# A product moved from VectorE to GpSimd, and the last values of a layer in one go, in a four-layer sparse graph network

## The chip, the cores and the metric

The kernel runs on one core of a Trainium2 chip. The metric is the device time of the whole program in microseconds, the median over several executions. One further execution was recorded by the hardware profiler; durations of single instructions come from it.

## The reference

The input is a matrix of 3327 nodes by 256 features and an adjacency matrix of 3327 x 3327 integers, of which about one in 208 is 1. Four layers follow each other, all with the same adjacency. Layer 0:

```
h = x @ Wt.T + bt                              # 64 features
s = leaky_relu(h @ Wa.T + ba, 0.2)
w = softmax(where(adj > 0, s, NEG), axis=1)
y = x + (w @ h) @ Wp.T + bp
x = gamma * layernorm(y) + beta
```

Layers 1 to 3, each with its own weights, 8 heads of 32:

```
q, k, v = layernorm(x) @ w_qkv
attn = softmax(where(adj != 0, q @ k.T * SCALE, -inf))
x = x + (attn @ v) @ w_proj + b_proj
x = x + gelu(layernorm(x) @ w1 + b1) @ w2 + b2     # 1024 inner features
```

## The kernel before

The nodes are 26 blocks of 128 rows (the last is short), in groups of four. The work has two phases.

**Layer 0 with the lists (0 to about 500 us).** For every block, SyncE loads 128 rows of the adjacency as integers (`load`), ScalarE turns them into bf16 zeros and ones (`sign`, L714, after a one-column MEMSET of the padding, L711, on VectorE for the first three blocks and on GpSimd from then on), TensorE transposes them and ScalarE copies the transposes (`turn`, L723 and L724), and TensorE multiplies h with them (`sums`). From the same bf16 rows VectorE makes the lists of neighbours: `candidates` multiplies the row by the numbers 1 to 208 within each of 16 segments (L731, the product `v` of 128 x 3328, two buffers), takes the eight largest of each segment (L735, 16 MAX8), and `list` adds the segment's offset to those that are above zero (L741, L742) and draws the 40 largest by five MAX8 and four MATCH_REPLACE8 (L746, L748). The groups' own steps (`copy`, `back`, `soft`, `mix`, `project`, `add`, `norm`, `norm1`, `turn1`, `qkv`, `store`) are laid out by hand in a table `plan` of two places for each block; the loop issues, for block i, the load and sign of block i+2, the even place of the plan, `candidates(i)`, the turn of block i+2, the odd place, and `list(i)`. `soft` begins with a count and a comparison that writes `OH` (L892). Each engine runs its instructions in the order in which the code issues them.

**Layers 1 to 3.** The nodes are sorted by degree, so block 0 has lists of 40 and the others of 24 down to 10 (`CAPS`). `ORDER` takes them alternately from both ends, and block 0 last. `CHUNK` joins them in chunks of 3, then fours, then 2 and at last block 0 alone. Each block is cut in groups of four list places. GpSimd issues one indirect DMA for each place (L1303), which fetches 128 rows of keys and values of 2 KB; ten groups are in flight (`NBUF`). On VectorE a group's `scores` are a product and a reduction (L1325, L1326); after the last group of a block `softmax` takes the maximum and ScalarE the exponent (L1340), and the next block's q is copied by ScalarE (L1311). A group's `values` are a product on VectorE (L1366, three buffers `vw`) that TensorE adds up by transposing matmuls (L1372). Values run a set number of groups behind their block's last scores:

```
for _ in range(2 if len(todo) > NBUF // 2 or b == 0 else 1):
    if todo and wait[todo[0][0]] > 1:
        value()
self.some()
```

`some` issues steps of the rest: `short` are those of one block (copy of the transposes L1390, projection L1396, `add` L1400), `long` those of a chunk, in the order in which chunks become due (normalisation, `up` L1439, `gelu` L1445, `down` L1462, `shift`, `back`, `add` L1480, and, if there is a next layer, its normalisation, q, k and v L1492, and `keep` L1498 to L1500, which copies k and v, scales q, and stores k and v). A rate sets how many `long` steps one call issues. After the scores of the last block the remaining values are drained with a call of `some` after each, then all steps that are left. The next layer's first gather waits until all k and v are stored.

Of the kernel before, what the change touches and what calls it, by code (L numbers as in the profile page):

```python
# [8 lines left out]
FP = mybir.dt.float32  # L9
BF = mybir.dt.bfloat16  # L10
I32 = mybir.dt.int32
AF = mybir.ActivationFunctionType
ALU = mybir.AluOpType
# [4 lines left out]
P = 128  # L18
N = 3327
D = 256  # L20
HEADS = 8
# [11 lines left out]
NB = (N + P - 1) // P  # L33
# [16 lines left out]
NSEG = 16  # L50
SEG = NB * P // NSEG
# [472 lines left out]
def sparse_path(ctx, tc, ins, out, dram, flag):  # L524
    nc = tc.nc
    const = ctx.enter_context(tc.tile_pool(name="s_const", bufs=1))
    small = ctx.enter_context(tc.tile_pool(name="s_small", bufs=4))

    ident = const.tile([P, P], FP, name="s_ident")
# [12 lines left out]
    kv = {1: dram.tile([PADDED + 1, KVW[1]], FP, name="kv1"),  # L542
          2: dram.tile([PADDED, KVW[2]], FP, name="kv2"),
          3: dram.tile([PADDED, KVW[3]], FP, name="kv3")}
# [78 lines left out]
    with tc.tile_pool(name="a", bufs=1) as a, tc.tile_pool(name="aw", bufs=2) as aw, \  # L623
# [10 lines left out]
        seg1 = a.tile([P, SEG], BF, name="seg1")  # L634
# [13 lines left out]
        num = a.tile([P, P], FP, name="num")  # L648
# [3 lines left out]
        part = a.tile([P, 1], FP, name="part")  # L652
# [27 lines left out]
        nd = LMAX + 1  # L680
# [3 lines left out]
        OH = a.tile([P, NB, nd], BF, name="OH")  # L684
# [9 lines left out]
        class Block:  # L694
# [21 lines left out]
            def turn(self, aT):  # L716

                i = self.i
                for k0 in range(0, NB, 7):
# [3 lines left out]
                        nc.tensor.transpose(pt[:, m, :], self.abf[:, k * P:(k + 1) * P], ident_bf)  # L723
                    nc.scalar.copy(aT[:, k0:k0 + len(ks), :], pt[:, :len(ks), :])  # L724

            def candidates(self, part=None):

                i = self.i
                if not part:
                    v = self.v = aw.tile([P, NSEG, SEG], BF, tag="v", name=f"s_v_{i}")  # L730
                    nc.vector.tensor_mul(v, self.abf.rearrange("p (s c) -> p s c", c=SEG),  # L731
                                         seg1[:, None, :].to_broadcast([P, NSEG, SEG]))
                    self.cand = aw.tile([P, NSEG, 8], FP, tag="cand", name=f"cand_{i}")
                for s in range(NSEG) if part is None else range(part * 4, part * 4 + 4):
                    nc.vector.max(out=self.cand[:, s, :], in_=self.v[:, s, :])  # L735

            def list(self):

                i, cand = self.i, self.cand
                tmp = aw.tile([P, NSEG, 8], FP, tag="ctmp", name=f"ctmp_{i}")  # L740
                nc.vector.scalar_tensor_tensor(tmp, cand, 0.0, off, ALU.is_gt, ALU.mult)  # L741
                nc.vector.tensor_add(tmp, cand, tmp)  # L742
                c2 = tmp.rearrange("p a b -> p (a b)")
                for k in range(0, LMAX, 8):
                    top = lists[:, i, k:k + 8]
                    nc.vector.max(out=top, in_=c2)  # L746
                    if k + 8 < LMAX:
                        nc.vector.match_replace(out=c2, in_to_replace=top, in_values=c2,  # L748
                                                imm_value=0.0)
# [91 lines left out]
        class Group:  # L841
# [36 lines left out]
            def soft(self):  # L878


                g, n, b0 = self.g, self.n, self.blocks[0]

                def sv(name):
                    t = aw.tile([P, 4], FP, tag="s_" + name, bufs=1, name=f"s_{name}_{g}")
                    return t[:, :n]

                sg = S.s[:, b0:b0 + n]
                dg = deg[:, b0:b0 + n]
                nc.vector.tensor_copy(dg, self.acc[:, :n, H0])
                top = sv("top")  # L890
                nc.vector.tensor_scalar(top, dg, float(LMAX), None, ALU.min)
                nc.vector.tensor_tensor(OH[:, b0:b0 + n, :],  # L892
                                        num[:, None, :nd].to_broadcast([P, n, nd]),
                                        top[:, :, None].to_broadcast([P, n, nd]), ALU.is_equal)

                at = places[:, :4 * nd].rearrange("p (b k) -> p b k", k=nd)
                for j in range(n):
                    i = b0 + j
                    add = [(tri, i)] + [(ones_bf, k) for k in range(b0, i)]
                    if g:  # L900
                        add += [(rest_tri, i - 4)] + [(ones_bf, k) for k in range(i - 3, b0)]
                    for lhsT, m in add:
                        nc.tensor.matmul(at[:, j, :], lhsT, OH[:, m, :], start=False, stop=True,
                                         skip_group_check=True)
                non, ga, fa, m1, m0, tt, mx = (
                    sv(k) for k in ("non", "ga", "fa", "m1", "m0", "tt", "mx"))
                nc.vector.tensor_scalar(non, dg, -1.0, float(N), ALU.mult, ALU.add)
                nc.vector.tensor_scalar(ga, dg, 0.0, None, ALU.is_gt)
                nc.vector.tensor_scalar(fa, non, 0.0, None, ALU.is_gt)
                nc.vector.tensor_scalar(tt, ga, -NEG0, NEG0, ALU.mult, ALU.add)  # L910
                nc.vector.tensor_mul(m1, sg, ga)
                nc.vector.tensor_add(m1, m1, tt)
                nc.vector.tensor_scalar(tt, fa, -1.0, 1.0, ALU.mult, ALU.add)
                nc.vector.tensor_mul(m0, sg, tt)
                nc.vector.scalar_tensor_tensor(m0, fa, NEG0, m0, ALU.mult, ALU.add)
                nc.vector.tensor_max(mx, m1, m0)
                nc.vector.tensor_sub(m1, m1, mx)
                nc.vector.tensor_sub(m0, m0, mx)
                nc.scalar.activation(m1, m1, AF.Exp)
                nc.scalar.activation(m0, m0, AF.Exp)  # L920
                self.non, self.m1, self.m0, self.tt = non, m1, m0, tt
# [107 lines left out]
        blk = [Block(i) for i in range(NB)]  # L1029
# [28 lines left out]
        for g in range(NG):  # L1058
            x_turn(g)
            if g:  # L1060
                h_of(g - 1)
            if g == 2:
                turn(3)
            if g == 4:
                blk[4].load()
                blk[4].sign()
            for _ in range(2 if g > 3 else 1):
                pieces.pop(0)()
        h_of(NG - 1)
# [34 lines left out]
        def step(g, name):  # L1104
            G = groups[g]
            G.qkv(int(name[3:])) if name[:3] == "qkv" else getattr(G, name)()

        for i in range(4, NB):
            if i + 2 < NB:
                blk[i + 2].load()  # L1110
                blk[i + 2].sign()
            for s in plan[2 * i]:
                step(*s)
            blk[i].candidates()
            if i + 2 < NB:
                turn(i + 2)
                if i % 2 or i + 2 == NB - 1:
                    sums(i + 2)
            for s in plan[2 * i + 1]:
                step(*s)  # L1120
            blk[i].list()
# [77 lines left out]
        top = a.tile([1, nd], FP, name="top")  # L1199
# [77 lines left out]
    class Layer:  # L1277
# [133 lines left out]
        def chunk(self, blocks, n2):  # L1411
            L, w, nxt = self.L, self.w, self.nxt
            n = len(blocks) * P
            b0 = blocks[0]
            x = [t2[:, b, :D] for b in blocks]
            js = range(len(blocks))
            c = {}
# [77 lines left out]
            def keep(j):  # L1495
                b = blocks[j]
                kvr = work.tile([P, 2 * D], FP, tag="kvr", name=f"kvr_{L}_{b}")
                nc.scalar.copy(kvr, c["pk", j])  # L1498
                nc.scalar.mul(t2[:, b, D:2 * D], c["pq", j][:, :D], -HD ** -0.5)
                nc.scalar.dma_start(kv[L + 1][b * P:(b + 1) * P, :], kvr)  # L1500

            def store(j):
                b = blocks[j]
# [50 lines left out]
                self.short.pop(0)()  # L1554

        def run(self):
            for _ in range(NBUF):
                self.issue()
            self.take_q(ORDER[0])

            todo, wait = [], {}

            def value():
                if todo[0][1] == 0:
                    self.weights(todo[0][0])
                self.values(*todo.pop(0))

            for k, b in enumerate(ORDER):
                for g in slots[b]:
                    self.scores(*g)  # L1570
                    if g == slots[b][-1]:
                        self.softmax(b)
                        if k + 1 < NB:
                            self.take_q(ORDER[k + 1])
                    for i in wait:
                        wait[i] += 1
                    for _ in range(2 if len(todo) > NBUF // 2 or b == 0 else 1):
                        if todo and wait[todo[0][0]] > 1:
                            value()
                    self.some()  # L1580
                todo += slots[b]
                wait[b] = 0
            while todo:
                value()
                self.some()
            self.rate = 4.0
            while self.short or self.long:
                self.some()
# [45 lines left out]
```

## Time and profile before

| | us |
|---|---|
| median of 3 runs | 3145.98 (3143.37 to 3151.08) |
| the profiled execution | 3158.07 |
| its span, first to last instruction | 3156.3 |
| VectorE busy | 1935.3 (61%) |
| TensorE busy, mean granted clock | 1794.0 (57%), 0.735 |
| GpSimd busy | 1362.7 (43%) |
| ScalarE busy | 774.6 (25%) |
| gathers of GpSimd (L1303) | 1344 of 947 ns |

Shares are averages over stages with different limits: in the first 500 us GpSimd has next to nothing to do, and in the layers it issues gathers. What a change in one stage is worth is read from that stage alone. A matmul's end is modelled[...].

### The profile page before, as it was taken

The numbers are of one execution on the slowest core, as the hardware profiler recorded it, in microseconds if no ns is written. First come the engines' busy times: TensorE is split into PE (matmuls) and PEld (weight loads), VectorE is DVE, ScalarE is ACT, GpSimd is POOL, SyncE is SP. The second block draws the span as 40 slices with busy tenths as digits, with TensorE's granted clock in tenths as the row PEclk, the third lists the DMA queues.
The fourth block names the chain that finished last, engine by engine and source line by source line (L and its number), as shares of the span: only waits on it lengthen the run. The fifth ranks groups of instructions, "written<-read, shape, count | busy, mean of one in ns | idle before, by whom it ended". The sixth has DMA issues, their size and how long they took to land.

```text
span 3156.3 us, 24036 instructions
## 1 busy us (share of the span) xinstructions
PE 1794.0 (57%) x7561; PEld 1163.5 (37%) x7561; DVE 1935.3 (61%) x3983; ACT 774.6 (25%) x1316; POOL 1362.7 (43%) x1458
## 2 busy tenths in 40 slices
PE   4767752255666666671457667666713435665556
PEld 3645531133333333350334333433512323433334
DVE  6688995457657656533656756755446556656554
ACT  4455621012222222230112212222300111212112
POOL 4000004545555554305555555544054555565550
PEclk9868766577787886785578778878755766776768
DMA  5334306645555565415455555555064554554560
GB/s 207 131 117 148 129 31 204 174 138 169 165 172 162 156 174 152 112 51 177 141 156 156 163 160 150 175 152 140 24 189 125 156 155 135 169 163 147 161 156 13
DMA packets 144486, 453.80 MB, mean 144 GB/s; under 512 B 29521, under 2 KB 40156, under 8 KB 141021
## 3 DMA queue, kind: packets, MB, share of 16 engines
q0 software_dynamic: 113056, 370.26, 40.9%
q1 hardware_dynamic: 9834, 53.90, 4.9%
q10 hardware_dynamic: 21458, 28.02, 2.5%
q8 instruction: 61, 1.00, 0.1%
q14 instruction: 77, 0.63, 0.1%
HBM read 420.64 MB, written 31.42 MB: 143 GB/s over the span
## 4 chain that ended last, share of the span: by engine, by line
DVE 25%; issue 18%; PE 18%; another core or an unknown queue 17%; POOL 11%; ACT 5%; DMA 5%; DVEq 0%; ACTq 0%; POOLq 0%; SPq 0%
POOL kv L1303 11%; DVE kv L1325 5%; DMA kv<-kv,t 4%; DVE sc L1326 3%; DVE vw L1366 3%; PE pu L1439 3%; PE po L1372 3%; PE py L1462 2%; DVE cand L735 2%; PE pk L1492 1%; PE s_pk L1010 1%; ACT s_aT L724 1%; DVE s_v L731 1%; PE pf L591 1%
## 5 line engine op out<-in xcount | busy, mean ns | idle before, releaser
L1303 POOL DMA_INDIRECT kv<-kv,t x1344 | 1273.0, 947 | 1210.3 <-issue 534.2
L1372 PE MATMUL po<-s_ident,vw 128*128 128x128 f32 x2688 | 475.4, 334 | 580.2 <-DVE vw L1366 387.2
L1372 PEld LDWEIGHTS po<-s_ident,vw 128*128 128x128 f32 x2688 | 395.5, 174 | 724.1 <-issue 373.5
L1325 DVE TENSOR_TENSOR kv<-kv,q 128x1024 f32<-128x1024 f32 (+3 forms) x363 | 413.1, 1138 | 397.1 <-ACT q L1311 274.6
L1366 DVE TENSOR_TENSOR vw<-kv,w 128x1024 f32<-128x1024 f32 x333 | 371.4, 1128 | 87.2 <-remote 84.6
L1326 DVE TENSOR_REDUCE sc<-kv 128x32 f32<-128x1024 f32 (+3 forms) x363 | 414.1, 1141 | 12.4
L1439 PE MATMUL pu<-fT,s_w 128*128 128x512 f32 (+3 forms) x768 | 341.2, 579 | 62.3 <-issue 35.8
L1462 PE MATMUL py<-gT,s_w 128*128 128x512 f32 (+2 forms) x672 | 321.8, 597 | 58.1 <-issue 50.2
L1400 DVE TENSOR_TENSOR t<-t,po 128x256 f32<-128x256 f32 x78 | 32.6, 418 | 390.8 <-remote 254.5
L1445 ACT ACTIVATE gT<-pu,pvb 128x512 f32<-128x512 f32 (+3 forms) x192 | 115.7, 607 | 628.2 <-remote 384.1
L1439 PEld LDWEIGHTS pu<-fT,s_w 128*128 128x128 f32 x768 | 157.4, 222 | 196.1 <-issue 146.4
L1462 PEld LDWEIGHTS py<-gT,s_w 128*128 128x128 f32 x672 | 132.6, 206 | 180.7 <-issue 144.0
L1396 PEld LDWEIGHTS po<-s_w_proj,oT 128*128 128x128 f32 x312 | 71.8, 255 | 281.8 <-issue 272.3
L1394 PE MATMUL po<-bias,s_ones_bf 96*128 96x256 bf16 x78 | 25.2, 324 | 259.7 <-issue 147.4
L1390 ACT COPY oT<-po 128x256 f32<-128x256 f32 x78 | 28.9, 371 | 548.5 <-remote 320.2
L711 POOL MEMSET s_abf<- 128x1 bf16 x23 | 2.2, 104 | 361.4 <-DVE s_v L731 253.7
L1492 PE MATMUL pk<-s_w_qkv,nT 128*128 128x512 f32 x208 | 128.4, 748 | 22.0 <-ACT nT L596 9.9
L735 DVE MAX8 cand<-s_v 128x8 f32<-128x208 bf16 x416 | 118.0, 360 | 0.9
L1396 PE MATMUL po<-s_w_proj,oT 128*128 128x256 f32 x312 | 113.1, 500 | 0.0
L723 PE MATMUL s_ptb<-s_ident_bf,s_abf 128*128 128x128 bf16 x676 | 67.1, 265 | 68.3 <-ACT s_abf L714 45.2
L591 PE MATMUL pf<-s_ident,xn_f 128*128 128x128 f32 x156 | 46.1, 444 | 86.8 <-ACT xn_f L588 66.7
L855 PE MATMUL s_pa<-s_aT,s_hs 128*128 128x256 bf16 x338 | 82.3, 290 | 13.2 <-DVE s_hs L817 13.2
(288 smaller groups left out, 2252.1 us busy)
## 6 DMA issues: line engine op xcount, KB each, us to landing
s_a<-in_adj_dram SPq DMA_DIRECT2D x25, 1663.5 KB
kv<-kv,t POOLq DMA_INDIRECT x1344
kv<-kvr ACTq DMA_DIRECT2D x52, 256.0 KB
kv<-s_kvr ACTq DMA_DIRECT2D x26, 256.0 KB
s_w<-in_L_gnn_w_dram SPq DMA_DIRECT2D x6, 1024.0 KB
t<-ql ACTq DMA_DIRECT2D x6, 592.0 KB
t<-s_x ACTq DMA_DIRECT2D x6, 512.0 KB
s_w_qkv<-in_L_gnn_w_qkv_dram SPq DMA_DIRECT2D x3, 768.0 KB
```

The source lines that it names most:

```text
L735: nc.vector.max(out=self.cand[:, s, :], in_=self.v[:, s, :])
L855: nc.tensor.matmul(self.pa[:, c0:c0 + 2 * P], S.hs[:r, k, :P], aT[:r, k, :], start=(k == 0), stop=(k == NB - 1))
L1303: nc.gpsimd.indirect_dma_start(out=t[:, s, :], out_offset=None, in_=kv[L], in_offset=bass.IndirectOffsetOnAxis(ap=t2[:, b, k:k + 1].bitcas ...
L1325: nc.vector.tensor_mul(k, k, self.q[b][:, None, :].to_broadcast([P, n, D]))
L1326: nc.vector.tensor_reduce(self.sc[b][:, s0:s0 + n, :], k.rearrange("p s (h d) -> p s h d", d=HD), AX.X, ALU.add)
L1366: nc.vector.tensor_mul(vw[:, :n * D].rearrange("p (s h d) -> p s h d", h=HEADS, d=HD), v, self.wp[b][:, s0:s0 + n, :, None].to_broadcast([ ...
L1372: nc.tensor.matmul(self.po[b][:, k * P:(k + 1) * P], vw[:, at:at + P], ident, is_transpose=True, start=(s0 + s == 0 and k == 0), stop=(s0 ...
L1396: nc.tensor.matmul(ps, c["oT"][:, k * P:(k + 1) * P], w["w_proj"][:, k, :], start=False, stop=(k == 1))
L1439: nc.tensor.matmul(c["pu", f][:, :n], w["w1"][:, e, f * P:(f + 1) * P], c["hT"][:, e, :n], start=(e == 0), stop=(e == 1))
L1445: nc.scalar.activation(g[:, :n], c.pop(("pu", f))[:, :n], AF.Gelu_apprx_tanh, bias=w["b1"][:, f:f + 1])
L1462: nc.tensor.matmul(c["py"][e][:, :n], w["w2"][:, f, e * P:(e + 1) * P], g[:, :n], start=(f == 0), stop=last)
L1492: nc.tensor.matmul(ps[:, :c1 - c0], c["hT"][:, e, j * P:(j + 1) * P], nxt["w_qkv"][:, e, c0:c1], start=(e == 0), stop=(e == 1))
```

## The change

In layer 0, the product `v` gets a function of its own, `weigh(engine)`. Blocks 0 to 3 keep it on VectorE inside `candidates`. Block 4's is issued on GpSimd in the pass over h, and in the main loop the one of block i+1 is issued on GpSimd right after the load and sign of block i+2, thus one block before its candidates. Two VectorE instructions take another form with the same result: the add in `list` (L742) and the comparison that writes `OH` (L892) become scalar_tensor_tensor.

In the layers, the values that are left after the last scores are issued without `some` between them; before them ScalarE gets one small activation with Gelu. In layer 3 a block's values start one group after its softmax instead of two. In `keep` the store of k and v is issued before the scaling of q. The chunks stay as they are.

```diff
+            def weigh(self, engine):
+                v = self.v = aw.tile([P, NSEG, SEG], BF, tag="v", name=f"s_v_{self.i}")
+                engine.tensor_mul(v, self.abf.rearrange("p (s c) -> p s c", c=SEG),
+                                  seg1[:, None, :].to_broadcast([P, NSEG, SEG]))
+
             def candidates(self, part=None):
                 i = self.i
+                if i < 4 and not part:
+                    self.weigh(nc.vector)
                 if not part:
-                    v = self.v = aw.tile([P, NSEG, SEG], BF, tag="v", name=f"s_v_{i}")
-                    nc.vector.tensor_mul(v, self.abf.rearrange("p (s c) -> p s c", c=SEG),
-                                         seg1[:, None, :].to_broadcast([P, NSEG, SEG]))
                     self.cand = aw.tile([P, NSEG, 8], FP, tag="cand", name=f"cand_{i}")
...
                 nc.vector.scalar_tensor_tensor(tmp, cand, 0.0, off, ALU.is_gt, ALU.mult)
-                nc.vector.tensor_add(tmp, cand, tmp)
+                nc.vector.scalar_tensor_tensor(tmp, cand, 0.0, tmp, ALU.add, ALU.add)
...
-                nc.vector.tensor_tensor(OH[:, b0:b0 + n, :],
-                                        num[:, None, :nd].to_broadcast([P, n, nd]),
-                                        top[:, :, None].to_broadcast([P, n, nd]), ALU.is_equal)
+                nc.vector.scalar_tensor_tensor(OH[:, b0:b0 + n, :],
+                                               num[:, None, :nd].to_broadcast([P, n, nd]), 0.0,
+                                               top[:, :, None].to_broadcast([P, n, nd]),
+                                               ALU.add, ALU.is_equal)
...
                 blk[4].load()
                 blk[4].sign()
+                blk[4].weigh(nc.gpsimd)
...
                 blk[i + 2].load()
                 blk[i + 2].sign()
+            if i + 1 < NB:
+                blk[i + 1].weigh(nc.gpsimd)
             for s in plan[2 * i]:
                 step(*s)
...
                 nc.scalar.copy(kvr, c["pk", j])
+                nc.scalar.dma_start(kv[L + 1][b * P:(b + 1) * P, :], kvr)
                 nc.scalar.mul(t2[:, b, D:2 * D], c["pq", j][:, :D], -HD ** -0.5)
-                nc.scalar.dma_start(kv[L + 1][b * P:(b + 1) * P, :], kvr)
...
+            behind = 2 if self.nxt else 1
...
-                        if todo and wait[todo[0][0]] > 1:
+                        if todo and wait[todo[0][0]] >= behind:
                             value()
...
+            table = small.tile([P, HEADS], FP, tag="table", name=f"table_{L}")
+            nc.scalar.activation(table, ident[:, :HEADS], AF.Gelu_apprx_tanh)
             while todo:
                 value()
-                self.some()
```

More of the change, by code (lines that the diff above doesn't have):

```diff
@@ L1556, in run @@
         def run(self):
+            L = self.L
             for _ in range(NBUF):
```

## The prediction

> **What bounds the kernel now.** I read the table of stages first, then in each stage that the diff touches the waits, the chain of work, and the instructions in order of time. The table by stretches of time (stretch, length, then busy time and count of PE, PEld, DVE, ACT, POOL, then granted TensorE clock, DMA share, GB/s):
>
> ```profile
> core 0: us, PE busy (x) PEld busy (x) DVE busy (x) ACT busy (x) POOL busy (x), PEclk, DMA share, GB/s
> ...
> 300.00:350.00 50.00, 33.98 (x236) 25.65 (x234) 47.02 (x173) 30.95 (x37) 0.30 (x3) 0.76 0.38 136
> 350.00:400.00 50.00, 37.19 (x284) 29.94 (x282) 46.48 (x169) 29.29 (x37) 0.30 (x3) 0.84 0.37 112
> ...
> 1330.00:1400.00 70.00, 51.77 (x217) 37.55 (x217) 33.14 (x77) 22.23 (x43) 0.00 (x0) 0.79 0.06 23
> ```
>
> In layer 0 (to about 500 us) VectorE works 47 us of 50 and GpSimd nothing. At the end of a layer (1330 to 1400) no DMA matters, PE leads and VectorE idles half the time. Inside the layers PE at a clock of 0.68 to 0.8, VectorE and waits between them share the bound. The waits of VectorE from 137 to 467 us (total, times, longest) confirm layer 0: 14 us in 330.
>
> ```profile
> DVE s_x L972 <- PE s_pp L963: 6.8, 3, 5.0
> DVE s_z L938 <- ACT s_m L919: 3.2, 1, 3.2
> DVE place L927 <- PE places L903: 2.7, 1, 2.7
> DVE s_x L986 <- ACT s_x L980: 1.5, 1, 1.5
> ```
>
> The groups by form in layer 0 (count | busy us, mean ns | idle before) price what moves; the two MEMSETs are all that GpSimd does there:
>
> ```profile
> L735 DVE MAX8 cand<-s_v 128x8 f32<-128x208 bf16 x326 | 92.2, 360 | 0.7
> ...
> L731 DVE TENSOR_TENSOR s_v<-s_abf,seg 128x3328 bf16<-128x3328 bf16 x20 | 37.6, 1882 | 0.0
> ...
> L742 DVE TENSOR_TENSOR ctmp<-cand,ctmp 128x128 f32<-128x128 f32 x20 | 5.8, 292 | 0.7
> L741 DVE SCALAR_TENSOR_TENSOR ctmp<-cand,off 128x128 f32<-128x128 f32 x20 | 5.8, 290 | 0.5
> ...
> L713 POOL MEMSET s_abf<- 32x3328 bf16 x1 | 2.9, 2866 | 0.1
> ```
>
> The last is the ends of layers, in order of time on VectorE (start, duration, then in brackets the idle time and who ended it), of layer 3:
>
> ```profile
> 3104.34 2.36 DVE L1366 TENSOR_TENSOR vw<-kv,sc 128x1024 f32<-128x1024 f32 x2
> 3115.55 0.75 DVE L1480 TENSOR_TENSOR t<-t,pd 128x256 f32<-128x256 f32 x2 [8.85 <-PE pd L1476]
> 3116.22 9.23 DVE L1366 TENSOR_TENSOR vw<-kv,sc 128x1024 f32<-128x1024 f32 x8
> ```
>
> Two value products of the last block run, then VectorE stands 8.85 us behind an `add` of the feed-forward chunk before it, then the other eight run. Layers 1 and 2 show the same with 16.7 and 16.5 us.
>
> **What the Trainium skill says.** "GPSIMD Engine Reference", section on performance versus the Vector engine: a two-input elementwise operation of 2048 fp32 elements takes 4497 ns on GpSimd, 2293 ns on VectorE. No run here shows a two-input operation on GpSimd; the one-input MEMSET above (0.86 ns an element) is the nearest row. "SBUF — State Buffer", section "Who interferes with whom": a VectorE instruction with two SBUF inputs and a GpSimd instruction that reads SBUF exclude each other; the second to start waits until the first has ended. The trace has no such pair, so it neither agrees nor disagrees: the gathers of the layers keep 0.95 us beside VectorE's two-input operations, but they are no elementwise reads. "ScalarE: Activation LUTs", section on what a table load costs: the trace agrees, with 1.28 us a load.
>
> **The change, part by part.** The profiled execution took 3158.07 us (span 3156.3, 1.8 around it); the median of the runs is 3145.98, 12.1 lower. I take differences against the profiled one and subtract them from the median.
>
> *Products to GpSimd.* VectorE loses 22 products (blocks 4 to 25) of 1.88 us: 41.4 us. GpSimd gains 22. Estimate from the skill's price: 3328 x 2.196 ns = 7.3 us each. From below, two inputs at the MEMSET's rate: 5.7 us; if bf16 streams as on VectorE, perhaps 4. Blocks 6 to 25 follow each other every 16.5 us, so even 7.3 us fits once per block. The queue of GpSimd has only the one-column MEMSETs (0.10 us) ahead; a MEMSET that waited for VectorE's product (229 us in sum) now waits for GpSimd's own, which is earlier, so signs and adjacency loads can only come forward. A product of block k starts when both `v` buffers allow it (the MAX8s of block k-2 have ended) and its sign is done; in the trace the former comes last for 16 of blocks 6 to 25. Until the MAX8s of block k there are then a list (3.8), the MAX8s of k-1 (4.5), another list (3.8) and the steps: at least 12 us on VectorE, so the first MAX8 does not wait. How much of 41 us shows? The chain of work from 130 to 470 us has this product at 6.9% of 340 us, 23 us; beyond that MAX8, s_pk and aT copies of other chains take over. From 137 to 467 us ACT is busy 171 of 330 and PE 218, so neither forbids a stage shorter by 25 us. I take -25, ends -12 (half of the 23 taken over by those chains) and -38 (nearly all 41). The new wait is that of the first MAX8 on GpSimd; behind it on VectorE are queued the list of the block and the steps of the groups, on which ACT and PE wait, so if the 12 us of cover are gone each us late is a us lost. The product of block 4 runs during the first pass over h, where GpSimd has nothing else.
>
> *Two scalar_tensor_tensor forms.* L741 against L742 above: 290 and 292 ns at one size. 22 and 7 instructions: zero in themselves, hidden or not. What they may do to the exclusion is in the first rival.
>
> *Last values in one go.* In layers 1 and 2 the drain starts with two `up` steps issued. Layer 2 before: from the first value's transposes (2239.65) to the last block's normalised input (xn_f, 2280.16) 40.5 us. After: ten values at 1.15 us (VectorE 1.17, PE 1.09, three `vw` buffers) 11.5; the rest of the feed-forward, 13.1 us on PE less two values of 1.04, 11.0; the last block's projection between them 1.0; transposing back 1.4; normalisation 4.7; turn 2.75; q, k, v and copies 6.2: 38.6. The last block's own projection, add and statistics (5.3) now lie beside it. So -2 for each of layers 1 and 2; the added serial order could as well cost 3. Layer 3: PE is through with feed-forward at about 3110 plus the last `down`s, then ten values to about 3123.5 instead of 3126.6: -3, from -6 to +2. The table load for Gelu is asked for where the next ACT operation is a Gelu anyway (3104.10 follows the load of 3102.80): nothing to win, one activation of about 0.2 us lost behind the exponent, covered by ten values.
>
> *Layer 3 one group behind.* A value then runs after one group of the next block instead of two. It needs the exponent, and ACT issues the next block's q copy behind that exponent; VectorE's first scores wait for that q already (68.1 us in 12 waits in layer 3). So no new wait. Ring buffers come free one group earlier: GpSimd's gathers are issued earlier, but VectorE waits for gathers only 16.8 us there. PE's transposes change places with feed-forward steps, the order of which the trace of before cannot price; at the end one group (2.4 us of scores) is won, in the middle as much can be lost: I take 0, from +5 to -8.
>
> *The keep step.* The store of 256 KB is issued before the 0.38 us scaling, whose issue (0.33) then stands ahead of that scaling on ACT. Only the last block's store delays a layer: 0.3 us in two layers at most, taken at 0; elsewhere nothing, as PE's next q, k, v matmuls (2.6 us) cover ACT. Without that cover each of the 52 would lose the 0.33.
>
> Sum: -25 - 2 - 2 - 3 = -32 on 3158.07, so 3126 profiled, and 3146 - 32 = **3114** for the median. Own range of this case: 3090 to 3132.
>
> **Rivals.** *The product locks VectorE out.* Where the product starts as the MAX8s end, L741 gets in first (0.03 us later), GpSimd takes the interface behind it, and the second form (0.33 us later, two SBUF inputs like L742) or OH in `soft` stands until the product ends: up to 7 us a block. Against the saving of 1.88 us it decides from a mean stall of 1.9 us a block on. At 6 us: 22 x 6 = 132, less 41, less some 10 of idle that absorb it: +81, with the ends' -7 +74: about 3220. At 3.5 us (half the product): 77 - 41 - 10 - 7 = +19: 3165. For it: the skill's rule names two SBUF inputs, not an opcode. Against: that the rule holds for this other form is not in the trace, and a list's remaining 3.2 us have one input each. *Nothing gained in layer 0*: ACT copies and PE take over as bound, or stalls of about 2 us a block just eat the saving; the ends alone (-7) give 3139. *The ends go the other way* (the last block's chain behind that of two blocks before): +6 instead of -7, which shifts any case by 13.
>
> **How the numbers follow.** Forecast 0.50, lock-out 0.38, nothing gained 0.12 (half of it just faster by more than 0.3%, which is 9.4 us and about what this measurement can tell). So faster 0.54, same 0.07, slower 0.39. The range reaches from 3092 (best clean case) to 3225 (most of the lock-out).
>
> **What would show it.** Right: the product's row on POOL with 4 to 8 us, L742 and L892 in their new form at 0.3 us, candidates of successive blocks some 15 us apart; no 16 us idle before L1480 in layers 1 and 2. Wrong: rows of two-input VectorE operations (ctmp, OH, s_m, s_x) with means of microseconds in layer 0, and block spacing above 18 us.

## The result, and the profile after

| | before | after |
|---|---|---|
| median, us | 3144.68 (3142.17 to 3151.08, 4 runs) | 3195.86 (3188.06 to 3200.01, 4 runs) |
| ratio | | 1.0157 [1.0132, 1.0182] |
| profiled execution, us | 3158.07 | 3195.98 (span 3194.2) |
| VectorE busy, us | 1935.3 | 2004.9 |
| GpSimd busy, us | 1362.7 | 1506.3 |
| first gather of layer 1, us | 509.5 | 570.4 |

The change costs 51 us; 3114 was forecast. The first gather, which ends layer 0, comes 60.9 us later. From it to the end the profiled execution takes 23.0 us less (2646.8 before, 2623.8 after), but the profiled execution of before was 13.4 us above its median and that of after is at its median. About 10 us of gain remain for the layers. So all of the loss lies in layer 0.

The table by stretches of time of the changed kernel, with the columns shown before (busy us and count of PE, PEld, DVE, ACT, POOL, then clock, DMA share, GB/s):

```profile
300.00:350.00 50.00, 30.66 (x173) 21.01 (x174) 48.08 (x131) 22.46 (x28) 17.61 (x5) 0.70 0.33 112
350.00:400.00 50.00, 30.27 (x207) 23.73 (x206) 47.53 (x132) 25.18 (x32) 15.04 (x6) 0.74 0.33 114
```

The busy column of VectorE looks better than before (48 of 50 us instead of 47), yet its count has fallen from 173 and 169 instructions to 131 and 132, and PE's and ACT's with it. An instruction that stands, that is, does not get on after its recorded start, is counted as busy: the rows below show one of 0.29 us recorded with 6.45. Read the count beside the busy time, and then the mean by form. VectorE's groups by form, 110 to 500 us (count | busy us, mean ns | idle before):

```profile
L740 DVE MAX8 cand<-s_v 128x8 f32<-128x208 bf16 x320 | 90.2, 359 | 20.0 <-POOL s_abf L711 20.0
L748 DVE SCALAR_TENSOR_TENSOR ctmp<-cand,ctmp 128x128 f32<-128x128 f32 x20 | 79.7, 3987 | 0.7
L898 DVE SCALAR_TENSOR_TENSOR OH<-num,s_top 128x164 bf16<-128x164 f32 x6 | 32.9, 5479 | 0.2
...
L746 DVE SCALAR_TENSOR_TENSOR ctmp<-cand,off 128x128 f32<-128x128 f32 x20 | 5.8, 290 | 0.5
```

In the profile before, OH was this row (110 to 450 us):

```profile
L892 DVE TENSOR_TENSOR OH<-num,s_top 128x164 bf16<-128x164 f32 x6 | 2.0, 330 | 0.2
```

The list's second instruction, called its second form from here on (L742 before, L748 now), went from 292 to 3987 ns, and OH (L892, now L898) from 0.33 to 5.48 us, while the list's first form and MAX8 are unchanged. These means are mixtures. One by one, 12 of the second forms take 6.43 to 6.46 us and the others 0.29; five of the `OH` take 6.49 to 6.53 and the others 0.24 to 0.33. That is 12 x 6.16 + 5 x 6.18 = 104.8 us of standing. The page gives the product's row:

```profile
L729 POOL TENSOR_TENSOR s_v<-s_abf,seg 128x3328 bf16<-128x3328 bf16 x22 | 142.6, 6484 | 296.5 <-DVE cand L740 160.3
```

The product takes 6.48 us, and most of GpSimd's idle time before it is ended by the last MAX8 of the block two before, as the prediction argued from the two `v` buffers. One block in order of time (start, duration, then the instruction; a line joins repeats):

```profile
288.72 0.64 DVE L740 MAX8 cand<-s_v 128x8 f32<-128x208 bf16 x2
289.39 0.29 DVE L746 SCALAR_TENSOR_TENSOR ctmp<-cand,off 128x128 f32<-128x128 f32 x1
289.53 6.49 POOL L729 TENSOR_TENSOR s_v<-s_abf,seg 128x3328 bf16<-128x3328 bf16 x1 [13.82 <-DVE cand L740]
289.72 6.45 DVE L748 SCALAR_TENSOR_TENSOR ctmp<-cand,ctmp 128x128 f32<-128x128 f32 x1
...
296.20 0.29 DVE L752 MAX8 lists<-ctmp 128x8 f32<-128x128 f32 x1
```

The first form gets in 0.14 us ahead of the product; the second starts 0.19 us after it and ends with it. No wait is recorded: VectorE has no idle time here, its instruction is just 22 times as long. The table of waits of VectorE from 137 to 500 us shows the same from the other side (total, times, longest):

```profile
DVE s_z L945 <- ACT s_m L926: 3.3, 1, 3.3
DVE place L934 <- PE places L910: 1.1, 1, 1.1
DVE s_x L979 <- issue: 0.2, 1, 0.2
```

Before, VectorE waited 14.2 us for others; now 4.6 (up to 528 us, where the same work ends, no row is added). The 9.6 us between are what the slower VectorE absorbed. With smaller standings (4.2 us of block 3's product, which VectorE still makes; 1.9 of L945; 1.1 of a COPY) the standing is 112.0 us; less 22 x 1.88 = 41.4 it is +70.6, against VectorE's measured +69.6; less 9.6 it is about the 60.9 by which layer 0 grew. Counted up to the first gather, VectorE is busy 69.9 us longer (472.7 against 402.8) and idle 8.9 us less (97.8 against 106.7). Candidates of blocks 6 to 25 follow each other every 19.1 us instead of 16.3 (the prediction read 16.5).

The end of layer 1 on VectorE, first a row of before, then the rows after:

```profile
1378.07 0.42 DVE L1480 TENSOR_TENSOR t<-t,pd 128x256 f32<-128x256 f32 x1 [16.69 <-PE pd L1476]
```

```profile
1416.69 3.50 DVE L1376 TENSOR_TENSOR vw<-kv,sc 128x1024 f32<-128x1024 f32 x3
1421.74 8.03 DVE L1376 TENSOR_TENSOR vw<-kv,sc 128x1024 f32<-128x1024 f32 x7 [1.55 <-PE po L1382]
1435.46 0.42 DVE L1410 TENSOR_TENSOR t<-t,po 128x256 f32<-128x256 f32 x1 [5.69 <-PE po L1406]
...
1445.13 0.42 DVE L1490 TENSOR_TENSOR t<-t,pd 128x256 f32<-128x256 f32 x1 [8.58 <-PE pd L1486]
```

The ten values now run with one pause of 1.55 us for a `vw` buffer, and the `add` of the feed-forward chunk (L1480, now L1490), for which VectorE waited 16.69 us between them, comes behind them with 8.58 us of idle. Not all of that idle time is gone: the same `add` for the last block, at the end of the layer, waits 18.19 us for TensorE (at 1470.34 us) where it waited 10.70 before, so the two waits together are 26.8 us instead of 27.4.

### The profile page after: what moved, and what is told of

The parts are those of the page before. It is cut to its first block, busy times and chain, and to the rows that moved or that the text cites. A ratio compares the mean times of both kernels' runs of the same rounds, so it can differ in the third digit from the quotient of the medians.

```text
span 3194.2 us, 24065 instructions
## 1 busy us (share of the span) xinstructions
PE 1829.6 (57%) x7561; PEld 1184.4 (37%) x7561; DVE 2004.9 (63%) x3961; ACT 775.6 (24%) x1319; POOL 1506.3 (47%) x1480
## 4 chain that ended last, share of the span: by engine, by line
PE 14%; issue 12%; DVE 11%; another core or an unknown queue 9%; POOL 7%; ACT 3%; DMA 2%; DVEq 0%; ACTq 0%; POOLq 0%; SPq 0%
POOL kv L1313 7%; PE pu L1449 4%; PE py L1472 3%; PE po L1382 3%; DVE kv L1335 3%; DVE vw L1376 2%; DVE sc L1336 2%; DMA kv<-kv,t 2%; PE pk L1502 1%; PE po L1406 1%; ACT L1350 1%; ACT gT L1455 1%; DVE t L1490 1%; PE pf L591 0%
## 5 line engine op out<-in xcount | busy, mean ns | idle before, releaser
L1382 PE MATMUL po<-s_ident,vw 128*128 128x128 f32 x2688 | 490.4, 339 | 596.1 <-DVE vw L1376 388.2
L1382 PEld LDWEIGHTS po<-s_ident,vw 128*128 128x128 f32 x2688 | 403.0, 176 | 747.2 <-DVE vw L1376 390.5
L729 POOL TENSOR_TENSOR s_v<-s_abf,seg 128x3328 bf16<-128x3328 bf16 x22 | 142.6, 6484 | 296.5 <-DVE cand L740 160.3
L723 PEld LDWEIGHTS <-s_abf 128*128 128x128 bf16 x676 | 60.1, 128 | 97.0 <-ACT s_abf L714 70.5
```

The source lines that it names most:

```text
L729: engine.tensor_mul(v, self.abf.rearrange("p (s c) -> p s c", c=SEG), seg1[:, None, :].to_broadcast([P, NSEG, SEG]))
L1382: nc.tensor.matmul(self.po[b][:, k * P:(k + 1) * P], vw[:, at:at + P], ident, is_transpose=True, start=(s0 + s == 0 and k == 0), stop=(s0 ...
```

## Experiments

Each kernel is compared with the kernel before on the same chip in the same series. The chips differ: before took 2570.15 us in the first series (experiments 1 to 4), 3123.18 in the second (5 to 7) and 2568.73 in the third (8). Layer 0 is alike on all (it ends at 503 to 513 us with the code of before); the difference lies in the layers, so differences in us are compared within a series only. First gathers and layer lengths are from single profiled executions.

**1. The parts of the layers alone.** Layer 0 of before, the layers of the change.

> The kernel before with only the parts in the layers: remaining values in one go with the small Gelu activation, layer 3 one group behind, the store in keep ahead of the scaling. Layer 0 is as before, its first gather at about 509.5 us. In the profile of the whole change the first gather is 60.9 us later and the end 37.9 us later, so the layers are 23 us shorter there (6.5, 1.1 and 15.5 us in layers 1, 2, 3); by the medians (+51) only some 10. Theory A (these parts gain, mostly by the lag in layer 3): 10 to 20 us less than before, 3125 to 3135, layer 3 from its first gather to the end 835 instead of 850.5. Theory B (as predicted, lag worth nothing): 7 less, 3138. Theory C (the shorter layers are only a shifted clock, the parts themselves cost): 0 to +6, 3145 to 3151.

Measured: 2564.30, ratio 0.9975 [0.9964, 0.9986], 5.9 us less. This is theory B: the ends gain about what they were forecast to gain (7). From gather to gather, against pool_alone in the same series (layers as before), layers 1, 2 and 3 are 3.3, 0.9 and 5.3 us shorter. The split by layer is not clear of scatter: pool_tensor_tensor (experiment 3), whose layers are the same code as pool_alone's, has a layer 3 that is 3.0 us shorter than pool_alone's. Most of the 23 us of the first comparison were thus the long profiled execution of before.

**2. The product on GpSimd alone.** Layer 0 of the change, the layers of before.

> The kernel before with only the products of blocks 4 to 25 on GpSimd and the two scalar_tensor_tensor forms; the layers as before. Lock-out theory: the second form of the list has a mean near 4.0 us and OH near 5.5 us, layer 0 ends 61 us later, and the whole is 60 us slower than before, about 3205. If the loss came from the layers instead, it is within 10 us of before, 3135 to 3155.

Measured: 2627.51, ratio 1.0219 [1.0204, 1.0234], 57.4 us more; first gather at 562.4, 59.4 after ends_alone's 503.0. The second form has a mean of 3987 ns and OH of 5477, as in the whole change. So the loss is layer 0's, of the size and in the two places that were expected. 57.4 - 5.9 = 51.5 is the whole change's 51.2, though that was measured on another chip.

**3. Does the form of the instruction matter?**

```diff
-                nc.vector.scalar_tensor_tensor(tmp, cand, 0.0, tmp, ALU.add, ALU.add)
+                nc.vector.tensor_add(tmp, cand, tmp)
...
-                nc.vector.scalar_tensor_tensor(OH[:, b0:b0 + n, :], ..., 0.0, ..., ALU.add, ALU.is_equal)
+                nc.vector.tensor_tensor(OH[:, b0:b0 + n, :], ..., ..., ALU.is_equal)
```

> As pool_alone, but the add of the list and the comparison for OH stay tensor_tensor as in the kernel before. Theory 1 (what counts is two SBUF inputs, not the form of the instruction): the add has a mean near 4.0 us and OH near 5.5 us, the time is that of pool_alone within 6 us, about 3205. Theory 2 (the scalar_tensor_tensor form is what is locked out): the add back at 0.29 us and OH at 0.32 us, time near 3120. Theory 3 (the form softens the lock-out, since the first form runs without a stall): the add longer than 4.0 us by a us or more, 3225 or above.

Measured: 2628.30, ratio 1.0219 [1.0203, 1.0236]. The groups by form, VectorE, 110 to 500 us:

```profile
L748 DVE TENSOR_TENSOR ctmp<-cand,ctmp 128x128 f32<-128x128 f32 x20 | 79.8, 3988 | 0.7
L898 DVE TENSOR_TENSOR OH<-num,s_top 128x164 bf16<-128x164 f32 x6 | 32.9, 5476 | 0.2
```

3988 against 3987 ns: the form makes no difference, so theory 1 holds. The two times agree as well (2628.30 and 2627.51). The two rewritten instructions do nothing for or against the lock-out.

**4. One operand in PSUM.** PSUM is the memory into which this kernel's matmuls write; its other tiles lie in SBUF.

```diff
+                raised = places[:, 384:].rearrange("p (a b) -> p a b", b=8)
-                nc.vector.scalar_tensor_tensor(tmp, cand, 0.0, off, ALU.is_gt, ALU.mult)
+                nc.vector.scalar_tensor_tensor(raised, cand, 0.0, off, ALU.is_gt, ALU.mult)
-                nc.vector.scalar_tensor_tensor(tmp, cand, 0.0, tmp, ALU.add, ALU.add)
+                nc.vector.scalar_tensor_tensor(tmp, cand, 0.0, raised, ALU.add, ALU.add)
```

> As the whole change, but the first form of the list writes its result to PSUM (free columns of the bank of places), so the second form reads one operand from SBUF and one from PSUM. OH keeps its two SBUF inputs. Lock-out by two SBUF inputs: the second form goes from 3.99 to about 0.35 us, which takes 20 x 3.6 = 73 us off; what comes back is that later two-input instructions (after the list's further 3.2 us) meet the last 2.7 us of the product, 0 to 50 us: 3123 to 3175, likeliest 3150. Rival (VectorE and GpSimd contend whatever the operands, or it waits for something else that ends with the product): the second form stays near 4 us and the time near 3196.

Measured: 2576.18, ratio 1.0020 [1.0013, 1.0028], 6.0 us more than before and about 45 less than the sum of 1 and 2, where 46 less was likeliest. The same groups:

```profile
L899 DVE SCALAR_TENSOR_TENSOR OH<-num,s_top 128x164 bf16<-128x164 f32 x6 | 26.7, 4451 | 0.2
...
L994 DVE TENSOR_TENSOR s_x<-s_x,s_brow 128x1024 f32<-128x1024 f32 x6 | 16.3, 2725 | 1.9 <-ACT s_x L988 1.9
...
L747 DVE SCALAR_TENSOR_TENSOR places<-cand,off 128x128 f32<-128x128 f32 x21 | 6.3, 298 | 29.3 <-PE places L911 28.8
L749 DVE SCALAR_TENSOR_TENSOR ctmp<-cand,places 128x128 f32<-128x128 f32 x21 | 6.0, 287 | 0.7
```

With one SBUF operand the second form takes 0.29 us every time, also the 12 times that it starts 0.20 us behind the start of the same product. The trace has a second case: L980 adds `s_x` to `s_pp`, which lies in PSUM; 10 of these adds start inside a product and take 0.67 to 0.69 us, as outside. What keeps two SBUF inputs (OH, and now L994, 1.22 us when nothing holds it) still stands. The 28.8 us ahead of L747 are a wait of this experiment's own making: it shares its PSUM tile with matmuls.

**5. GpSimd with one input.** `tensor_copy` of the row in place of the product.

> As the whole change, but GpSimd copies the block's row instead of multiplying it by the numbers 1 to 208: the weighting of blocks 4 to 25 is left out, so their lists and the rows that the layers fetch are others, and only layer 0 is read. GpSimd then reads one SBUF operand instead of two. Theory 1 (a GpSimd instruction that reads SBUF excludes a two-input VectorE instruction, whatever its own number of inputs): the second form of the list stands as long as the copy runs, mean about 0.6 of the copy's duration (3.99 against 6.48 in the whole change). Theory 2 (two inputs are needed on both sides): the second form and OH back at 0.3 us.

The groups by form, VectorE and then GpSimd, 110 to 500 us (GpSimd to 560):

```profile
L751 DVE SCALAR_TENSOR_TENSOR ctmp<-cand,ctmp 128x128 f32<-128x128 f32 x21 | 35.1, 1672 | 0.7
...
L901 DVE SCALAR_TENSOR_TENSOR OH<-num,s_top 128x164 bf16<-128x164 f32 x6 | 12.6, 2099 | 0.2
```

```profile
L730 POOL COPY s_v<-s_abf 128x3328 bf16<-128x3328 bf16 x21 | 62.4, 2972 | 292.2 <-DVE cand L743 148.2 <-ACT s_abf L714 61.4 <-DVE deg L898 34.5
```

The copy takes 2.97 us, and 11 second forms take 2.93 us: the mean is 0.56 of the copy's duration. Theory 1 holds: on GpSimd's side one SBUF input is enough. The standing follows the length of what GpSimd runs, 2.97 us here and 6.48 before. GpSimd has to read, though. Its one long MEMSET (32x3328, 2.87 us) only writes. In six of the profiles an instruction with two SBUF inputs starts inside it, and none stands: the list's second form takes 0.29 us five times (experiments 6 and 8), 0.08 to 0.09 us behind the MEMSET's recorded start, and L995 of experiment 4, the twin of L994, takes 1.23 us, 1.02 us behind it.

**6. The product beside the MAX8s.** A MEMSET of one element ties the start of GpSimd's product to the MAX8s; GpSimd takes `HALF` of the 16 segments, VectorE the rest.

```diff
+            def weigh(self, engine, s0=0, s1=NSEG):
...
+                    if engine is nc.gpsimd:
+                        nc.vector.memset(self.v[:, 0, :1], 0.0)
...
+            if HALF < NSEG:
+                blk[i].weigh(nc.vector, HALF)
+            if i + 1 < NB:
+                blk[i + 1].weigh(nc.gpsimd, 0, HALF)
             blk[i].candidates()
```

> As the whole change, but the product of block i+1 is held back until the 16 MAX8 of block i begin: a one-element MEMSET of its v by VectorE stands right ahead of them, and GpSimd's product overwrites that element. GpSimd takes 11 of the 16 segments (estimate 11/16 of 6.48 = 4.46 us, the 16 MAX8 take 4.5), VectorE the other 5 (estimate 5/16 of 1.88 = 0.59 us) before the MEMSET. Lock-out theory: MAX8 has one input, so nothing stands: the second form of the list is back at 0.3 us, OH at 0.33, MAX8 stays at 0.36 us, VectorE saves 1.88 - 0.59 - 0.1 = 1.2 us a block, 24 in all, of which half to all shows, and the ends give 6 more: 15 to 30 us less than the kernel before. Rival (any GpSimd product slows whatever VectorE does beside it): MAX8 rises above 0.4 us and the time is that of the kernel before or longer.

> The same, but GpSimd takes all 16 segments (6.48 us). Lock-out theory: the last 2.0 us of the product stick out behind the MAX8s and stop the next two-input instruction of VectorE, so the first form of the list or a step ahead of it is longer by up to 1.8 us in most blocks; VectorE saves 1.88 - 0.1 and loses about as much, so layer 0 ends within 10 us of the kernel before's, and the whole is 0 to 10 us less than before (ends 6). Rival (the MAX8s are slowed): worse than that by 20 us or more.

Measured with 11 segments: 3109.85, ratio 0.9954 [0.9935, 0.9973], 13.3 us less by the medians and so just short of the 15 to 30 expected. With 16: 3127.91, ratio 1.0016 [0.9988, 1.0043], no clear difference, where 0 to 10 us less was expected. VectorE's groups by form with 16 segments:

```profile
L751 DVE SCALAR_TENSOR_TENSOR ctmp<-cand,off 128x128 f32<-128x128 f32 x21 | 34.8, 1659 | 0.5
...
L900 DVE COPY deg<-s_acc 128x4 f32<-128x4 f32 x6 | 13.0, 2160 | 1.7 <-ACT s_acc L887 1.7
...
L753 DVE SCALAR_TENSOR_TENSOR ctmp<-cand,ctmp 128x128 f32<-128x128 f32 x21 | 6.1, 292 | 0.7
```

Now the first form stands (14 times about 2.35 us), because the product's last 2 us stick out behind the MAX8s, and the second is free again. The MAX8s keep 358 ns, with the product beside 298 of the 416, so the rival "GpSimd slows whatever runs beside it" falls. With 11 segments (4.52 us) the two forms of the list have means of 333 and 292 ns and OH 329.

**7. The lag of layer 3.**

> As ends_alone, but layer 3 keeps its values two groups behind. If all of the gain of ends_alone (0.25% or 6 us; layers 3.3, 0.9 and 5.3 us shorter than in pool_alone) comes from the values in one go, the time is that of ends_alone within 1 us. If the lag is what shortens layer 3, it is 3 to 5 us longer than ends_alone and layer 3 takes 678 to 680 us from its first gather to the end instead of 674.8.

Measured on the chip of the second series: 3113.61, ratio 0.9969 [0.9948, 0.9990], 9.6 us less than before; ends_alone, on the chip of the first series, had 5.9 less, so this does not decide. Its layer 3 took 824.5 us; under_max8_part and under_max8_whole, which have the lag change, took 831.1 and 831.4. The third series asks again with timed kernels side by side.

**8. Variants side by side.** part_alone has the layers of before; part_with_ends all of the change's; part_ends_no_lag `behind = 2` in layer 3 too. In the last, GpSimd takes all 16 segments and the order is changed:

```diff
-            blk[i].candidates()
...
-            blk[i].list()
+            blk[i].list(lambda: blk[i + 2].weigh(nc.gpsimd) if i + 2 < NB else None)
+            if i + 1 < NB:
+                blk[i + 1].candidates()
```

The function passed to `list` is called behind its second form.

> Layer 0 of under_max8_part (11 of 16 segments on GpSimd beside the MAX8s, 5 on VectorE ahead of them), the layers as in the kernel before. VectorE saves 24 us in layer 0; the first run showed the first gather 12.5 us earlier than in ends_without_lag on the same chip. If layer 0's gain is handed on whole: 12 us less than before (0.4%). If ScalarE and the matmul chains take it back: within 3 us of before.

> under_max8_part once more, now beside its variants on one chip. Additive: part_alone's gain and another 6 to 10 us for the ends, 18 to 22 us less than before. If the gain of 0.46% measured first is all there is, the two parts overlap and it is 14 us less.

> The same with layer 3 two groups behind as before. On the chip of the second series layer 3 took 824.5 us from its first gather to the end without the lag change and 831.1, 831.4 and 831.0 with it. If the lag costs that, this is 6 us faster than part_with_ends, 24 to 28 us less than before; if it is chance, the two are equal within 2 us.

> As part_ends_no_lag, but all 16 segments go to GpSimd and the candidates of block i+1 follow the list of block i at once, ahead of the steps of the groups; the product of block i+2 is released behind the list's second form, so 3.2 us of list and 4.5 us of MAX8, all with one input, lie beside its 6.48 us. Lock-out theory: no two-input form of list or OH above 0.35 us, VectorE saves a further 0.6 us a block, 12 us, half of it shown: 5 us faster than part_ends_no_lag. Rival (the steps of the groups now stand in one place instead of two for each block, so the chains through ScalarE and TensorE between them are waited for): VectorE's waits on TensorE and ScalarE grow by 20 us or more and it is slower than part_ends_no_lag.

| | median, us | ratio to before | first gather, us |
|---|---|---|---|
| part_alone | 2559.53 | 0.9963 [0.9950, 0.9976] | 494.2 |
| part_with_ends | 2553.00 | 0.9932 [0.9914, 0.9950] | 493.7 |
| part_ends_no_lag | 2552.99 | 0.9938 [0.9921, 0.9955] | 494.6 |
| under_list_and_max8 | 2547.68 | 0.9916 [0.9901, 0.9932] | 488.9 |

Layer 0 gains 9.2 us by the medians (12, or less than 3, had been expected) and the ends another 6.5. The two together, 15.7, lie between the 14 and the 18 to 22 of the two theories; 9.2 and ends_alone's 5.9 make 15.1, so the parts add up. The lag is worth nothing here: equal medians, and layer 3 takes 674.2 us with it and 674.4 without. That it cost some 6 us on the chip of the second series rests on single profiles of kernels with different layers 0. In their layers 3 VectorE has 12 idle stretches of over 8 us without the lag change and 12 and 14 with it, 178 us against 198 and 204, so 6 us lie within the scatter of these stretches; it stays open. The last kernel is the fastest of all, 21 us below before; its 5.3 us over part_ends_no_lag are as expected, though the two intervals against before overlap, and so do the runs (2544.2 to 2549.6 against 2548.3 to 2557.2).

How much of a saving shows? VectorE's part of the product has a median of 0.69 us, the MEMSET 0.06: 22 x (1.88 - 0.69 - 0.06) = 25 us should go. Two instructions at the start still stand, block 4's own part on VectorE (5.04 us) and block 3's whole product (4.10 instead of 1.89), which takes 6.6 us back. Up to the first gather VectorE is busy 384.1 us in part_ends_no_lag and 402.8 in ends_alone, which has the layer 0 of before: 18.7 less. Of these 8.4 show (first gather at 494.6 and 503.0). VectorE's waits of part_ends_no_lag from 137 to 494 us:

```profile
DVE s_x L984 <- PE s_pp L975: 14.5, 6, 6.3
DVE s_x L998 <- ACT s_x L992: 7.8, 2, 5.2
DVE s_z L950 <- ACT s_m L931: 5.5, 1, 5.5
...
DVE place L939 <- PE places L915: 2.7, 1, 2.7
```

With two smaller rows these are 35.7 us, where ends_alone has 25.3 over the same stage (137 to 503 us). So about 10 of the 18.7 us turned into waits, nearly all for the matmul and ScalarE chains of `project`, `norm` and `soft`.

## Why the prediction was wrong

*The step that failed* is "The new wait is that of the first MAX8 on GpSimd". With it the sum took -25 for the products and put the exclusion of VectorE by GpSimd at nothing, and the two rewritten instructions at "zero in themselves, hidden or not". The runs showed another wait in its place: L748 and OH, which have two SBUF inputs, stood 104.8 us behind products that had started just before them, while a first MAX8 had to wait in one block only. The durations are right where nothing holds an instruction (L746: 290 ns), but they came from a profile in which GpSimd stood still. The first rival named this mechanism and its place, and it is what happened. I set it at 0.38 behind the clean case's 0.50, with two arguments against it. One was that the rule for two SBUF inputs might not reach the scalar_tensor_tensor form; experiment 3 shows that it does, to a nanosecond. The other was that the 3.2 us that remain of a list have one input each; they did not matter, because the second form itself comes 0.19 us after the product's start. "SBUF — State Buffer", section "Who interferes with whom" in the Trainium skill speaks of VectorE's instructions with two SBUF inputs and of GpSimd instructions that read SBUF; it names `tensor_tensor`, but not scalar_tensor_tensor. Experiments 3, 4 and 5 agree with it. The order of start, which the prediction had worked out itself, fixed the victim.

*The rival's size.* It gave 3220 at a mean of 6 us a block and 3165 at 3.5. Measured: 17 of the 22 products caught one of the two instructions for 6.2 us, 4.8 as a mean over 22. In the rival's own sum that is 22 x 4.8 - 41 - 10 - 7 = +47, against +51 measured. Its "7 us a block" was the estimate of 7.3 us a product, which is 6.48; its 10 us of absorbed idle time were 9.6. The measured 3196 lies inside the stated range only because that range had been drawn wide enough to take in most of this rival; the forecast of 3114 is not supported by that.

*The product.* 41.4 us off VectorE: right. Its 6.48 us lie between the estimates of 5.7 and 7.3; the MEMSET behind the 5.7 is called one-input, but its row has no input, and the one-input copy of experiment 5 took 0.89 ns an element against its 0.86. "The first MAX8 does not wait": right except for block 5, whose MAX8s wait 20.0 us for GpSimd (11.3 before, ahead of the product on VectorE). There the cover is missing and the product's longer run, 6.48 instead of 1.88, shows. That signs "can only come forward" is wrong for this block: ScalarE begins its sign at 114.6 us instead of 105.0. *-25 of 41* was never tested in that form, as the lock-out came with it. The nearest measurements (experiment 8: 8.4 of 18.7 us show in part_ends_no_lag, 14.1 of 34.3 in under_list_and_max8) say that the share was taken too high; with these shares, 0.45 and 0.41, a clean case would have been at -17 to -19, an estimate.

*Last values in one go.* Forecast -2, -2, -3. part_ends_no_lag against part_alone has -3.4, -4.3 and -2.6 in single profiles and -6.5 by the medians. The sum is right. The split is not shown: layer 2, with one and the same code, took 688.6 us in part_with_ends and 685.3 in part_ends_no_lag. *Lag one group*: taken at 0; 0 in the third series. *Keep step*: 0, not tried by itself; it is inside the ends. The rival that the ends go the other way falls.

*What would show it*: of the signs of being wrong, ctmp and OH "with means of microseconds" and "block spacing above 18 us" came, at 4.0 and 5.5 us and at 19.1. `s_m` and `s_x` did not: in 17 of 22 cases the list or OH caught the product first. `s_x` stands when the list no longer does (L994 in experiment 4). Of the signs of being right, the product's row (6.48 us) came. "No 16 us idle before L1480" came for the feed-forward chunk (8.58), but the last block's `add` then has 18.19. The chances do not add up exactly: half of 0.12 on top of 0.50 is 0.56 for faster, not 0.54.

## What to carry to other kernels

Before work goes to GpSimd, list what VectorE issues during it, if the work reads SBUF. In these runs an instruction with two SBUF inputs that started inside GpSimd's product or copy stood to its end, from 128x4 to 128x3328 elements and in both forms, so the price of each is up to GpSimd's duration and not VectorE's saving. Tie GpSimd's start to a stretch of work that does not stand (here 4.5 us of MAX8, or 7.7 with the list) and cut it to that length, or put an operand in PSUM (which here brought 28.8 us of other waits with it). In a profile such a stall has no wait: look for a small form whose mean is a mixture, and for a count that falls while busy time stays.

## What the runs showed of the hardware that was not expected

- A COPY with one SBUF input stands too: `deg` (128x4 fp32 from SBUF to SBUF, 0.15 us alone in the changed kernel) took 2.33 to 2.38 us five times in under_max8_whole, and a TENSOR_SCALAR of 128x4 took 2.81 instead of 0.17 beside the copy of experiment 5. "SBUF — State Buffer", section "Who interferes with whom" lists copy and tensor_scalar among the forms that can contend; these traces agree. So two inputs are not needed for every form. MAX8, MATCH_REPLACE8 and BATCH_NORM_STATS2 in the same position kept their durations (358, 275 and 395 ns).
- Nothing is shared in part: GpSimd's product took 6.46 to 6.51 us whether a VectorE instruction stood behind it or MAX8s ran beside it, and the one that stood did its own work after it. OH (0.33 us alone) ended 0.18 us behind the product's end, L994 (1.22) 1.08 and block 3's product on VectorE (1.89) 1.75: each time its own length less 0.14 or 0.15 us. In all eleven kernels with the product or the copy on GpSimd, no VectorE instruction with two SBUF inputs, and no COPY or TENSOR_SCALAR, that started inside one of these ended before it, but for one that started 1 ns behind the copy.
- Chips differ by more than any change here: the same kernel takes 2569 and 2570 us on two and 3123 and 3145 on two others, nearly all of it in the layers. The profile shows a mean TensorE clock of 0.78 on the first two and 0.73 to 0.74 on the others; that 6% by itself does not account for 22%. In the layers, VectorE has 9 to 11 idle stretches of over 8 us on the first two chips, 105 to 125 us in sum. On the others it has 47 (ends_without_lag) and 56 (before), 712 and 820 us in sum. There 27 waits of VectorE, some 360 us, are ended by something that the profile does not show; ends_alone and part_alone, on the first two chips, have none. So the time goes into long waits, and their cause stays open.
